# Order of issue in a fused attention, cond2 and ffn kernel: fixed delays replaced by a clock of estimates, with finer parts and layer norm by pairs

## Chip, cores and metric

The kernel runs on one core of one Trainium2 chip. The metric is the device time of one execution in microseconds (us). The engines are TensorE (PE; its weight loads are listed as PEld), VectorE (DVE), ScalarE (ACT), GpSimd (POOL) and SyncE (SP), which here only issues DMAs. [...]

## What is computed

The input `x` is [8, 512, 256] in float32: eight images of T = 512 tokens with C = 256 channels. Cut to what matters, the reference is:

```python
y  = x @ weight[itok].T + bias[itok]             # per image, one of 8 weight sets
q, k, v = silu(y @ Wq), silu(y @ Wk), y @ Wv     # 16 heads of 16
q, k = lrpe(q), lrpe(k)                          # [t*cos, t*sin], 32 per head
o  = (tril(q @ k.T) @ v) @ Wo                    # linear attention, causal, no softmax
x  = x + layernorm(o * sigmoid(y @ G1 @ G2)) * gamma + beta

ctx   = ema(x, tau_ctx)                          # cond2: running averages along T
gated = x * sigmoid([x, ctx] @ Wg.T + bg)
mod   = 0.5 + sigmoid(gelu(x @ Wn1.T + bn1) @ Wn2.T + bn2)
temporal = sum_d softmax(blend)_d * ema(gated * mod_d, tau_d)     # D = 8 traces
c  = layernorm((gelu(x @ Wsoma.T + bsoma) * sigmoid(temporal @ Wtemp.T + btemp)) @ Wout.T)
c  = c * gamma + beta

g, u = bitlinear(c, w_gate), bitlinear(c, w_up)  # ffn, INNER = 1024
x  = x + bitlinear(silu(g) * u, w_down)          # rows quantised to 8 bit, weights to -1, 0, 1
```

## The kernel before

One image is worked on by three Python generators, which issue instructions and yield between parts: `attention(b)` (L248), `cond2(b)` (L650) and `ffn(b)` (L845). Two more, `setup_cond2` (L512) and `setup_ffn` (L623), prepare constants and quantised weights at the start. A main loop (from L891) resumes one generator at a time; in the steady state the attention of image b, cond2 of image b−1 and the ffn of image b−2 are all running, so that their instructions are mixed on every engine.

The names that the profile shows:

- *attention*: `pxT` (x transposed), `py` (y), then for each of four tiles of 128 tokens `pkq` and `pv` (projections), `ktok` and `qtok` (the rotation, on POOL), `pkT`, `pqT` (transposed) and `pst` (chunk states, summed into `total` on DVE). For each pair of tiles there are two groups of `pe` (energies; DVE multiplies by the causal mask into `et`), `po` (output, copied to `aT`) and `pw` (times Wo). `pg` and `pgt` make the gate. Then the layer norm: `og`, `bn`, `mv` on DVE, `rstd` on POOL (L243, L244), L503 and `x` (L506) on DVE. POOL adds beta to x once, early (L444).
- *cond2*: `px2T`, the scan `cT` (L660), `ph`, `pso` (soma), `pm` (mod), `pwg` (gated), `pc`, `pr`, then `ptr`: two k parts for each of two groups of four traces, each in one four-bank tile of PSUM, summed into `tempT` by four DVE instructions. After it `ptg`, `pwo`, and on DVE the layer norm and quantisation of `c2` in two pairs of tiles: L808, L814, L819, L840, `c_inv`, `steps`, L827 and L830, which writes `cq`. SP transposes `cq` into `cqT` by DMA.
- *ffn*: for each of four tiles two groups of `pw_gateT` and `pw_upT` (L858), `sig` on ACT, `h` on DVE (L862), then `hmax` (L864), scales, L868 and `hq` (L870), a DMA transpose to `hqT`, `pd` (L885), `res` (L887) and the store.

PSUM holds four banks that all these tiles share in rotation (pool `ps`) and one four-bank tile (pool `ps_t`, tag `ptr`). The SBUF pools `p1` to `p6` have as many buffers per name as their number says.

What sets the order is a clock that counts PE's work by hand-written figures. Each generator yields the time at which its next part is ready, as a fixed delay after that:

```python
    def spent(work, then):
        now[0] += work
        return now[0] + then
    ...
        ripe = [r for r in running if running[r][0] <= now[0]]
        rank = min(ripe) if ripe else min(running, key=lambda r: running[r][0])
```

Among the ripe generators ffn goes first, then cond2, then attention. The attention of image b+1 starts once image b has issued its second `po` (`tail[b]`). The order in which the loop issues is, but for small moves by the framework below, the order on each engine.

Of the kernel before, what the change touches and what calls it, by code (L numbers as in the profile page):

```python
# [15 lines left out]
P = 128  # L16
# [14 lines left out]

@with_exitstack
def adaln_attn_ffn_kernel(ctx: ExitStack, tc: tile.TileContext, a: dict, out: bass.AP):
# [13 lines left out]
    cp = ctx.enter_context(tc.tile_pool(name="const", bufs=1))  # L47
    ps = ctx.enter_context(tc.tile_pool(name="ps", bufs=4, space=bass.MemoryType.PSUM))
    ps_t = ctx.enter_context(tc.tile_pool(name="ps_t", bufs=1, space=bass.MemoryType.PSUM))
    p1 = ctx.enter_context(tc.tile_pool(name="p1", bufs=1))  # L50
    p2 = ctx.enter_context(tc.tile_pool(name="p2", bufs=2))
    p3 = ctx.enter_context(tc.tile_pool(name="p3", bufs=3))
    p4 = ctx.enter_context(tc.tile_pool(name="p4", bufs=4))
    p6 = ctx.enter_context(tc.tile_pool(name="p6", bufs=6))
# [10 lines left out]
    now = [0.0]  # L65

    def spent(work, then):

        now[0] += work
        return now[0] + then  # L70
# [5 lines left out]
    nc.vector.tensor_copy(ident_bf, ident)  # L76
    ones = cp.tile([P, P], F32, name="ones")
    nc.vector.memset(ones, 1.0)
    minus_half = cp.tile([P, 1], F32, name="minus_half")
    nc.vector.memset(minus_half, -0.5)  # L80

    causal = cp.tile([P, 64], F32, name="causal")
    for r in range(2):
        nc.gpsimd.affine_select(
            out=causal[64 * r : 64 * (r + 1), :],
            in_=ones[64 * r : 64 * (r + 1), :64],
            pattern=[[1, 64]],
            compare_op=ALU.is_ge,
            fill=0.0,
            base=0,  # L90
            channel_multiplier=-1,
        )

    own = cp.tile([P, 2, 2, HD], F32, name="own")
    nc.vector.memset(own, 0.0)
    for j in range(4):
        nc.vector.memset(own[32 * j : 32 * (j + 1), j // 2, j % 2, :], 1.0)
# [3 lines left out]
    nc.sync.dma_start(sid_t, a["sid"].rearrange("(o n) -> o n", o=1))  # L101

    def load_input(b):
        xs = p4.tile([P, NT, C], F32, tag="x", name=f"x_{b}")
        nc.sync.dma_start(xs, x[b].rearrange("(t p) c -> p t c", p=P))
        sid = nc.sync.value_load(sid_t[0:1, b : b + 1], min_val=0, max_val=NS - 1)
        wt = p1.tile([P, KC, C], F32, tag="wt", name=f"wt_{b}")
        nc.sync.dma_start(
            wt,
            a["weightT"].rearrange("s (k p) o -> s p k o", p=P)[bass.ds(sid, 1)].rearrange("s p k o -> (s p) k o"),  # L110
        )
        bt = p2.tile([P, KC], F32, tag="bt", name=f"bt_{b}")
        nc.sync.dma_start(bt, a["biasT"][bass.ds(sid, 1)].rearrange("s p k -> (s p) k"))
        return xs, wt, bt
# [4 lines left out]
    def load_w(name, src, eng=nc.sync):  # L119
        rows, cols = src.shape  # L120
        t = cp.tile([P, rows // P, cols], F32, name=name)
        eng.dma_start(t, src.rearrange("(k p) n -> p k n", p=P))
        return t

    def load_row(name, src):
        t = cp.tile([P, src.shape[0]], F32, name=name)
        nc.sync.dma_start(t, src.partition_broadcast(P))
# [3 lines left out]
    nc.scalar.dma_start(theta_c, a["theta_c"])  # L131

    wkq = cp.tile([P, KC, 2, C], F32, name="wkq")
    for i, n in enumerate(("wk", "wq")):
        nc.scalar.dma_start(wkq[:, :, i, :], a[n].rearrange("(k p) n -> p k n", p=P))
    wv = load_w("wv", a["wv"], eng=nc.scalar)
# [3 lines left out]
    nc.vector.memset(g1, 0.0)  # L140
    nc.sync.dma_start(g1[:, :, :HD], a["g1"].rearrange("(k p) n -> p k n", p=P))
    g2 = cp.tile([64, C], F32, name="g2")
    nc.vector.memset(g2, 0.0)
    for u in range(2):
        nc.sync.dma_start(g2[32 * u : 32 * u + HD, :], a["g2"])
# [6 lines left out]
    nc.sync.dma_start(tau, a["taus"].partition_broadcast(P))  # L152
    blend = p1.tile([D, C], F32, tag="blend", name="blend")
    nc.sync.dma_start(blend, a["blend"])
    raws = {}

    def load_raw(n, *places):
# [3 lines left out]
            pool.tile([P, half * cols], F32, tag=tag, name=f"{n}_raw_{s}") for s, (pool, tag) in enumerate(places)  # L161
        ]
        for s, raw in enumerate(raws[n]):
            nc.sync.dma_start(
# [10 lines left out]
    for s in range(2):  # L175
        nc.sync.dma_start(w["wn2"][HN * s : HN * (s + 1), :], a["wn2T"])
        nc.sync.dma_start(w["bn1"][HN * s : HN * (s + 1), :], a["bn1"].rearrange("(p o) -> p o", o=1))
    w["bn2"] = load_row("bn2", a["bn2"])
    for n in ("bsoma", "btemp"):
        w[n] = cp.tile([P, KC], F32, name=n)  # L180
        nc.sync.dma_start(w[n], a[n])
# [13 lines left out]
    for g in range(NG):  # L195
        nc.vector.tensor_scalar(diag[:, g, :], ident, theta_c[:, g : g + 1], None, ALU.mult)
    theta = bank("theta")
    nc.tensor.matmul(theta, ones, diag.rearrange("p g n -> p (g n)"), start=True, stop=True)
    posn = p1.tile([P, NT], F32, tag="posn", name="posn")
    nc.gpsimd.iota(posn, pattern=[[P, NT]], base=0, channel_multiplier=1, allow_small_or_imprecise_dtypes=True)  # L200
    half_pi = cp.tile([P, 1], F32, name="half_pi")
    nc.vector.memset(half_pi, HALF_PI)
    ang = p1.tile([P, NT, H, HD], F32, tag="soma", name="ang")
    for t in range(NT):
        nc.vector.tensor_scalar(
# [8 lines left out]
    nc.vector.tensor_scalar(turns, ang, INV_TWO_PI, MAGIC, ALU.mult, ALU.add)  # L214
    nc.vector.tensor_scalar(turns, turns, -MAGIC, None, ALU.add)
    for part in (TWO_PI_1, TWO_PI_2, TWO_PI_3):
        nc.vector.scalar_tensor_tensor(ang, turns, -part, ang, ALU.mult, ALU.add)
    nc.vector.tensor_scalar(ang, ang, PI_BELOW, -PI_BELOW, ALU.min, ALU.max)
    nc.vector.scalar_tensor_tensor(turns, ang, -1.0, ang, ALU.mult, ALU.max)
    cs = cp.tile([P, NT, NG * P], F32, name="cs")  # L220
    cs_by_head = cs.rearrange("p t (h e d) -> p (t h) e d", e=2, d=HD)
    nc.scalar.activation(cs_by_head[:, :, 1, :], ang.rearrange("p t h d -> p (t h) d"), AF.Sin)
    nc.scalar.activation(
# [6 lines left out]
    for i in range(3):  # L230
        vz = cp.tile([P, 2, H // 2, 4, HD], F32, name=f"vz{i}")
        nc.gpsimd.memset(vz, 0.0)
        vz_bufs.append(vz)

    def layer_stats(src, mv_row):
        st = p3.tile([P, nc.vector.BN_STATS_DIM], F32, tag="bn", name="bn")
        nc.vector.bn_stats(st, src)
        nc.vector.bn_aggr(mv_row, st)

    def layer_rstd(mv, name):  # L240

        r = p2.tile([P, NT], F32, tag="rstd", name=name)
        nc.gpsimd.tensor_scalar(r, mv[:, :, 1], 4.0 * EPS, None, ALU.add)  # L243
        nc.gpsimd.tensor_tensor(r, r, minus_half.to_broadcast([P, NT]), ALU.pow)  # L244
# [3 lines left out]
    def attention(b, xs, wt, bt):  # L248

        xT = p1.tile([P, KC, T], F32, tag="xT", name=f"xT_{b}")  # L250
        for k in range(KC):
            pt = bank(f"pxT_{b}_{k}")
            for t in range(NT):
                nc.tensor.transpose(pt[:, chunk(t)], xs[:, t, chunk(k)], ident)
            nc.scalar.copy(xT[:, k, :], pt)
        yield spent(1.1, 1.4)
        yT = p1.tile([P, KC, T], F32, tag="yT", name=f"yT_{b}")
        for o in range(KC):
            py = bank(f"py_{b}_{o}")
            for k in range(KC):  # L260
                nc.tensor.matmul(py, wt[:, k, chunk(o)], xT[:, k, :], start=k == 0, stop=k == KC - 1)  # L261
            nc.scalar.activation(yT[:, o, :], py, AF.Identity, bias=bt[:, o : o + 1])  # L262
        wt_free[0] = b + 1
        yield spent(3.7, 1.0)

        kTs, qTs, vzs, sgs = {}, {}, {}, {}

        def project(t):
# [3 lines left out]
            for k in range(KC):  # L272
                nc.tensor.matmul(  # L273
# [3 lines left out]
            for k in range(KC):  # L277
                nc.tensor.matmul(pv, yT[:, k, chunk(t)], wv[:, k, :], start=k == 0, stop=k == KC - 1)  # L278
            sg = p2.tile([P, 2, H, HD], F32, tag="sg", name=f"sg_{b}_{t}")
            nc.scalar.activation(sg.rearrange("p e h d -> p (e h d)"), pkq, AF.Silu)  # L280
# [4 lines left out]
            nc.scalar.copy(vzs[tp][:, u, :, 0:4:3, :], pv.rearrange("p (a e d) -> p a e d", e=2, d=HD))  # L285
            sgs[t] = sg
# [4 lines left out]
        def rotate(t, i):  # L291
# [3 lines left out]
            tok = p3.tile([P, NG * P], F32, tag="tok", name=f"{n}tok_{b}_{t}")  # L295
            nc.gpsimd.tensor_mul(  # L296
                tok.rearrange("p (h e d) -> p h e d", e=2, d=HD),
                sgs[t][:, i].unsqueeze(2).to_broadcast([P, H, 2, HD]),
                cs[:, t, :].rearrange("p (h e d) -> p h e d", e=2, d=HD),
            )  # L300
            pt = bank(f"p{n}T_{b}_{t}")
            for g in range(NG):
                nc.tensor.transpose(pt[:, chunk(g)], tok[:, chunk(g)], ident)  # L303
            nc.scalar.copy(turned[:, :, chunk(u)], pt.rearrange("p (g n) -> p g n", n=P))  # L304
            return tok

        def states(t, tok):
# [4 lines left out]
            for g in range(NG):  # L312
                for r, hh in ((0, 0), (1, 1), (0, 1), (1, 0)):
                    rows = slice(64 * r, 64 * (r + 1))
                    cols = slice(P * g + 64 * hh, P * g + 64 * (hh + 1))
                    nc.tensor.matmul(  # L316
# [6 lines left out]
            for r in range(2):  # L323
                c = 2 * t + r
                if c:
                    sts[c] = p6.tile([P, NG, 2, 2 * HD], F32, tag="st", name=f"st_{b}_{c}")
                    nc.gpsimd.tensor_mul(  # L327
# [8 lines left out]
                if c:  # L336
                    nc.vector.tensor_add(new, src, total[0])  # L337
                else:
                    nc.vector.tensor_copy(new, src)
# [4 lines left out]
        def energies(tp, hh):  # L344
# [3 lines left out]
            for g in range(NG):  # L348
                for u in range(2):
                    for e, r in ((0, 0), (1, 1), (0, 1), (1, 0)):  # L350
                        rows = slice(32 * (2 * hh + e), 32 * (2 * hh + e + 1))
                        at = slice(P * u + 64 * r, P * u + 64 * (r + 1))
                        nc.tensor.matmul(  # L353
                            pes[e][64 * r : 64 * (r + 1), g, u, :], kT[rows, g, at], qT[rows, g, at], start=True, stop=True
                        )
            for e in range(2):
                et = p4.tile([P, NG, 2, 64], F32, tag="et", name=f"et_{b}_{tp}_{2 * hh + e}")
                nc.vector.tensor_mul(  # L358
# [6 lines left out]
        def output(tp):  # L365
# [7 lines left out]
            def out(half, pair, u, r, *factors, last):  # L373
                q = 32 * pair
                nc.tensor.matmul(po[r][q : q + 32, half, u, :], *factors, start=(r, q) not in begun, stop=last)  # L375
# [28 lines left out]
            for r in range(2):  # L404
                nc.scalar.copy(aTs[tp].rearrange("p h (u r n) -> p h u r n", u=2, r=2)[:, :, :, r, :], po[r])  # L405

        ready = {}

        def projected(t):
            project(t)  # L410
            ready[t] = spent(2.9, 1.6)

        def turned(t):
            tok = rotate(t, 0)
            states(t, tok)
            spent(1.3, 0)
            rotate(t, 1)
            ready[t] = spent(0.6, 1.2)

        projected(0)  # L420
        yield now[0]
        projected(1)
        yield ready[0]
        turned(0)
        yield now[0]
        projected(2)
        yield ready[1]
        turned(1)
        yield ready[1]
        energies(0, 0)  # L430
        at = spent(1.2, 0)
        yield at
        projected(3)
        yield max(at, ready[2])
        turned(2)
        energies(0, 1)
        at = spent(1.2, 2.0)
        yield max(at, ready[3])
        while b and not done[b - 1, "attention"]:
            yield now[0] + 1.0  # L440
        output(0)
        turned(3)

        nc.gpsimd.tensor_add(xs, xs, beta_a.unsqueeze(1).to_broadcast([P, NT, C]))  # L444
        spent(2.0, 0)
        yield now[0]

        pg = bank(f"pg_{b}")[:64, : T // 2]
        for tp in range(NT // 2):
            for k in range(KC):  # L450
                for u in range(2):
                    nc.tensor.matmul(
# [7 lines left out]
        nc.scalar.copy(g1T, pg)  # L460
        at = spent(1.1, 0.8)
# [538 lines left out]
```

## Time and profile before

| what | value |
|---|---|
| median of the runs | 779.91 us |
| lowest, highest of 3 | 776.56, 782.77 us |
| the profiled execution | 779.86 us |
| its span, first to last instruction | 778.2 us |
| mean granted clock of TensorE | 0.930 |
| busy: PE, DVE, ACT, POOL | 665.8, 505.7, 260.5, 196.7 us |
| DMA | 28.64 MB, mean 37 GB/s |

The span is what the views divide; 1.66 us of the execution lie around it. The line PEclk cuts the span in 40 slices of 19.5 us and gives the granted clock in tenths (9 is 90% or more). A row of a waits view names the waiting engine with its tile and line, what it waited for, and then the total in us, the number of times and the longest. A row of the timeline gives the start, the duration, the instruction and, in brackets, how long its engine had been idle before it and what ended that.

### The profile page before, as it was taken

The numbers are of one execution on the slowest core, as the hardware profiler recorded it, in microseconds if no ns is written. First come the engines' busy times: TensorE is split into PE (matmuls) and PEld (weight loads), VectorE is DVE, ScalarE is ACT, GpSimd is POOL, SyncE is SP. The second block draws the span as 40 slices with busy tenths as digits, with TensorE's granted clock in tenths as the row PEclk, the third lists the DMA queues.
The fourth block names the chain that finished last, engine by engine and source line by source line (L and its number), as shares of the span: only waits on it lengthen the run. The fifth ranks groups of instructions, "written<-read, shape, count | busy, mean of one in ns | idle before, by whom it ended". The sixth has DMA issues, their size and how long they took to land.

```text
span 778.2 us, 21224 instructions
## 1 busy us (share of the span) xinstructions
PE 665.8 (86%) x9330; PEld 445.2 (57%) x9330; DVE 505.7 (65%) x1047; ACT 260.5 (33%) x480; POOL 196.7 (25%) x223
## 2 busy tenths in 40 slices
PE   2988999799888999799888999799988999795644
PEld 1566666566664666566664666466764667454312
DVE  3896355785567665775658753776658755785565
ACT  2822343243224333253234332253234333240111
POOL 3542252114301251023311152113411252110000
PEclk7969999999999999899999999999999999898756
DMA  6700000021001210022001210021000200021011
GB/s 229 231 3 3 14 2 4 15 67 56 4 16 32 56 37 3 15 63 60 4 15 21 69 35 4 16 49 48 3 16 6 69 9 3 16 55 28 1 41 54
DMA packets 61198, 28.64 MB, mean 37 GB/s; under 512 B 46346, under 2 KB 60594, under 8 KB 61106
## 3 DMA queue, kind: packets, MB, share of 16 engines
q1 hardware_dynamic: 60146, 26.50, 12.8%
q8 instruction: 73, 1.20, 0.6%
q10 hardware_dynamic: 960, 0.79, 0.3%
q14 instruction: 19, 0.16, 0.1%
HBM read 12.60 MB, written 4.19 MB: 22 GB/s over the span
## 4 chain that ended last, share of the span: by engine, by line
PE 67%; DVE 18%; issue 5%; ACT 4%; DMA 3%; POOL 3%; ACTq 0%; POOLq 0%; DVEq 0%; SPq 0%
PE pkq L273 7%; PE pwg L710 7%; PE ptr L760 5%; PE po L375 5%; PE ptg L778 4%; PE pso L682 4%; PE pv L278 3%; PE pd L885 3%; PE pe L353 3%; PE pwo L803 3%; PE pst L316 3%; PE py L261 3%; PE pw L491 2%; PE pqT L303 2%; PE pkT L303 2%
## 5 line engine op out<-in xcount | busy, mean ns | idle before, releaser
L765 DVE SCALAR_TENSOR_TENSOR tempT<-ptr,bw_c,tempT 128x512 f32<-128x512 f32 x128 | 95.8, 748 | 41.8 <-PE ptr L760 39.1
L861 ACT ACTIVATE sig<-pw_gateT,steps 128x512 f32<-128x512 f32 x64 | 43.2, 687 | 80.5 <-PE pw_gateT L858 45.9
L296 POOL TENSOR_TENSOR ktok<-sg,cs 128x512 f32<-128x512 f32 x32 | 41.2, 1286 | 108.2 <-ACT sg L280 94.9
L858 PE MATMUL pw_gateT<-w_gateT,cqT 128*128 128x512 bf16 x128 | 40.3, 398 | 31.4 <-DVE h L862 24.7
L273 PE MATMUL pkq<-wkq,yT 128*128 128x512 f32 x128 | 64.2, 622 | 0.3 <-ACT yT L262 0.3
L858 PEld LDWEIGHTS <-cqT 128*128 128x128 bf16 x256 | 25.9, 101 | 64.6 <-issue 35.9
L862 DVE SCALAR_TENSOR_TENSOR h<-pw_upT,steps,sig 128x512 f32<-128x512 f32 x64 | 45.9, 744 | 15.2 <-ACT sig L861 8.8
L375 PE MATMUL po<-et,vz 64*32 64x64 f32 x2048 | 32.0, 246 | 25.0 <-DVE et L358 15.7
L327 POOL TENSOR_TENSOR st<-total,own 128x256 f32<-128x256 f32 x56 | 41.2, 752 | 48.1 <-DVE total L337 48.1
L760 PE MATMUL ptr<-dm,gated 32*128 32x128 f32 x1024 | 40.6, 293 | 10.7 <-DVE tempT L765 10.7
L358 DVE TENSOR_TENSOR et<-pe,causal 128x512 f32<-128x512 f32 x64 | 41.8, 685 | 12.2 <-PE pe L353 12.2
L296 POOL TENSOR_TENSOR qtok<-sg,cs 128x512 f32<-128x512 f32 x32 | 40.8, 1277 | 32.7 <-PE pst L316 32.5
L885 PE MATMUL pd<-w_downT,hqT 128*128 128x256 bf16 x256 | 35.9, 288 | 14.5 <-DMA hqT<-hq 14.5
L760 PEld LDWEIGHTS ptr<-dm,gated 32*128 32x128 f32 x1024 | 33.9, 194 | 21.5 <-issue 19.5
L375 PEld LDWEIGHTS po<-et,vz 64*32 64x32 f32 x2048 | 25.0, 114 | 32.4 <-DVE et L358 19.0
L353 PE MATMUL pe<-qT,kT 32*64 32x64 f32 x2048 | 41.6, 223 | 1.3 <-ACT qT L304 0.9
L858 PE MATMUL pw_upT<-w_upT,cqT 128*128 128x512 bf16 x128 | 41.5, 408 | 1.3 <-ACT sig L861 1.3
L353 PEld LDWEIGHTS pe<-qT,kT 32*64 32x64 f32 x2048 | 35.7, 135 | 10.9 <-issue 4.1
L887 DVE SCALAR_TENSOR_TENSOR res<-pd,hstep,x 128x256 f32<-128x256 f32 x32 | 15.4, 482 | 40.7 <-PE pd L885 40.7
L885 PEld LDWEIGHTS <-hqT 128*128 128x128 bf16 x256 | 25.8, 103 | 27.5 <-DMA hqT<-hq 19.4
L405 ACT COPY aT<-po 128x256 f32<-128x256 f32 x32 | 10.5, 375 | 91.6 <-PE po L375 91.6
L864 DVE TENSOR_REDUCE hmax<-h 128x1 f32<-128x1024 f32 x32 | 38.9, 1216 | 0.3
(201 smaller groups left out, 1338.6 us busy)
## 6 DMA issues: line engine op xcount, KB each, us to landing
x<-in_x_dram SPq DMA_DIRECT2D x8, 512.0 KB, 4.3
out_dram<-res SPq DMA_DIRECT2D x32, 128.0 KB, 1.7
wt<-in_weightT_dram SPq DMA_DIRECT2D x8, 256.0 KB, 2.8
w_gateT_raw<-in_w_gateT_dram SPq DMA_DIRECT2D x2, 512.0 KB, 6.7
w_upT_raw<-in_w_upT_dram SPq DMA_DIRECT2D x2, 512.0 KB, 7.9
w_downT_raw<-in_w_downT_dram SPq DMA_DIRECT2D x2, 512.0 KB, 7.5
wgT<-in_wgT_dram SPq DMA_DIRECT2D x1, 512.0 KB, 8.7
hqT<-hq SPq DMA_TRANSPOSE x32, 2.7
```

The source lines that it names most:

```text
L273: nc.tensor.matmul(pkq, yT[:, k, chunk(t)], wkq[:, k].rearrange("p e c -> p (e c)"), start=k == 0, stop=k == KC - 1)
L296: nc.gpsimd.tensor_mul(tok.rearrange("p (h e d) -> p h e d", e=2, d=HD), sgs[t][:, i].unsqueeze(2).to_broadcast([P, H, 2, HD]), cs[:, t, : ...
L353: nc.tensor.matmul(pes[e][64 * r : 64 * (r + 1), g, u, :], kT[rows, g, at], qT[rows, g, at], start=True, stop=True)
L358: nc.vector.tensor_mul(et.rearrange("p g u n -> p (g u) n"), pes[e].rearrange("p g u n -> p (g u) n"), causal.unsqueeze(1).to_broadcast([P ...
L375: nc.tensor.matmul(po[r][q : q + 32, half, u, :], *factors, start=(r, q) not in begun, stop=last)
L710: nc.tensor.matmul(pwg[:, u, :], src[:, k % KC, chunk(t + u)], w["wgT"][:, k, :], start=k == 0, stop=k == 2 * KC - 1,)
L760: nc.tensor.matmul(ptr[:, r, :, t, :], gated[rows, t, chunk(k)], dm[rows, t], start=True, stop=True)
L765: nc.vector.scalar_tensor_tensor(acc, ptr[:, :, e].rearrange("p r t n -> p r (t n)"), w["bw_c"][:, k, d + e : d + e + 1], acc, ALU.mult, A ...
L858: nc.tensor.matmul(pm, cqT[:, t, k, :], w[n][:, k, cols], start=k == 0, stop=k == KC - 1)
L861: nc.scalar.activation(sig, pgu[0], AF.Silu, scale=steps[:, 0, t : t + 1])
L862: nc.vector.scalar_tensor_tensor(h[:, cols], pgu[1], steps[:, 1, t : t + 1], sig, ALU.mult, ALU.mult)
L885: nc.tensor.matmul(pd, hqT[:, k, :], w["w_downT"][:, k, :], start=k == 0, stop=k == KI - 1)
```

## The change

The computation stays as it is. `spent` and the fixed delays go. A class `Clock` estimates, for every instruction as it is issued, when it will start and end: it keeps a time for each engine (with the gaps left in it), for each area of each tile (last write and last use), for each buffer that a new tile takes over, for the DMA queue, for ACT's function tables[...]. `Engine` and `Pool` wrap the engines and the pools so that each call is accounted. A generator now yields a function that the main loop asks anew each time:

```diff
-    now = [0.0]
-    def spent(work, then):
-        now[0] += work
-        return now[0] + then
+    def needs(*aps, banks=(ps, "ps"), when=lambda: True):
+        def ready():
+            return max([clock.when(v) for v in aps] + [banks[0].free(banks[1])]) if when() else None
+        return ready
...
+        now = clock.at["tensor"]
+        ready = {r: v for r, v in ((r, running[r][0]()) for r in running) if v is not None}
+        ripe = [r for r in ready if ready[r] <= now]
+        rank = min(ripe) if ripe else min(ready, key=ready.get)
```

The ranks stay. The parts get finer: the turning of a tile in a k and a q part, `ptr` one k at a time, `ptg` and `pso` one output half at a time, `pwo` one pair of tiles at a time, `inner` (it was `hidden`) one group of gate and up at a time. In attention, the rotations follow at once on the projection (pool `p3` becomes `p4`), the layer norm is done by pairs of token tiles, and the first pair's `pw` stands ahead of the second `po`:

```diff
+            for i, n in enumerate("kq"):
+                toks[t, i] = tok = p4.tile([P, NG * P], F32, tag="tok", name=f"{n}tok_{b}_{t}")
+                gp.tensor_mul(
...
-        energies(1, 1)
-        yield spent(1.2, 2.0)
-        output(1)
-        at = spent(2.0, 0.9)
-        tail[b] = True
+        yield needs(kTs[1], qTs[1])
+        energies(1, 1)
         og = p1.tile([P, NT, C], F32, tag="og", name=f"og_{b}")
-        mv = p2.tile([P, NT, 2], F32, tag="mv", name=f"mv_{b}")
         for tp in range(NT // 2):
             t = 2 * tp
             if tp == 1:
-                yield at
+                yield needs(ets[1, 1, 1], sts[7])
+                output(1)
+                tail[b] = True
+            yield needs(aTs[tp])
...
+            mv = p2.tile([P, 2, 2], F32, tag="mv", name=f"mv_{b}_{t}")
...
-        rstd = layer_rstd(mv, f"rstd_a{b}")
-        for t in range(NT):
+            rstd = layer_rstd(mv, f"rstd_a{b}_{t}")
+            for u in range(2):
```

The next attention starts from the gate (`head[b]`, set once `pg` is copied) and waits for the tail only before it turns its second tile:

```diff
+        ac.copy(g1T, pg)
+        head[b] = True
...
-        if b < B and b in loaded and tail[b - 1]:
+        if b < B and b in loaded and head[b - 1]:
...
+        yield needs(toks[1, 0], when=lambda: tail[b - 1])
+        yield from turned(1)
```

In cond2 the products `dm` (L749) are issued next to `modt`, ahead of `gated`. In ffn the transpose to `hqT` follows directly on `hq`:

```diff
-            hqs[t] = hq, hstep, spent(2.1, 6.0)
...
-            hq, hstep, at = hqs.pop(t)
-            yield at
-            hqT = p2.tile([P, KI, P], BF, tag="hqT", name=f"hqT_{b}_{t}")
-            nc.sync.dma_start(hqT, hq, transpose=True)
-            yield spent(0.0, 4.0)
+            hqT = p2.tile([P, KI, P], BF, tag="hqT", name=f"hqT_{b}_{t}")
+            sy.dma_start(hqT, hq, transpose=True)
+            hqs[t] = hqT, hstep
...
+            hqT, hstep = hqs.pop(t)
+            yield needs(hqT)
```

Loops that polled for another generator (`while not ...: yield now[0] + 1.0`) become the `when` of such a function. In the two setups `paced` functions, which wait for DVE's estimate to come near, take the place of the fixed delays, and `blend` shares a buffer with `square`.

## The prediction

> **What bounds the kernel now.** I read section 1 of the page, then the windows for the three stages, then PE's waits, then the timeline of one turn of the steady stage.
>
> ```profile
> PE 665.8 (86%) x9330; PEld 445.2 (57%) x9330; DVE 505.7 (65%) x1047; ACT 260.5 (33%) x480; POOL 196.7 (25%) x223
> PEclk7969999999999999899999999999999999898756
> ...
> PE 67%; DVE 18%; issue 5%; ACT 4%; DMA 3%; POOL 3%; ACTq 0%; POOLq 0%; DVEq 0%; SPq 0%
> ```
>
> TensorE (PE) is busy 86% of the span, and the chain that ended last runs 67% on it; VectorE (DVE) comes next with 65% and 18%. The stages differ, which the windows show (PE, PEld, DVE, ACT, POOL busy, then clock, DMA share, GB/s):
>
> ```profile
> 0.00:144.00 144.00, 119.80 (x1990) 82.19 (x1991) 89.42 (x198) 53.33 (x100) 49.76 (x64) 0.92 0.22 68
> 144.00:672.00 528.00, 481.36 (x6986) 327.19 (x6985) 348.09 (x717) 184.74 (x342) 140.80 (x150) 0.96 0.12 29
> 672.00:778.00 106.00, 64.60 (x357) 35.87 (x355) 68.14 (x136) 22.41 (x38) 6.09 (x9) 0.78 0.13 33
> ```
>
> From the first gate matmul of image 0 (144) to that of image 6 (672) there are six turns of 88.0 us, in each of which one image's attention, another's cond2 and a third's ffn are mixed. PE idles 528.0 − 481.4 = 46.6 us there, 7.8 per turn. Eleven windows of 3.41 us at half clock cost at most 18.6 us of work, 3.1 per turn. So a turn holds 88.0 − 7.8 − 3.1 = 77.1 us of PE work at full clock: an order of issue has 10.9 us per turn to win, and any amount to lose. What PE waits for:
>
> ```profile
> PE pw_gateT L858 <- DVE h L862: 24.7, 7, 3.5
> PE po L375 <- DVE et L358: 15.7, 9, 1.9
> PE pd L885 <- DMA hqT<-hq: 14.5, 3, 6.7
> PE ptr L760 <- DVE tempT L765: 10.7, 5, 3.4
> PE po L375 <- issue: 9.5, 9, 2.3
> ```
>
> The first is one stall per turn, and the timeline shows its place:
>
> ```profile
> 588.94 0.37 POOL L243 TENSOR_SCALAR rstd_a<-mv 128x4 f32<-128x4 f32 x1 [12.40 <-DVE mv L238]
> 589.39 1.04 POOL L244 TENSOR_TENSOR rstd_a<-rstd_a,minus_half 128x4 f32<-128x4 f32 x1
> 590.46 1.28 DVE L506 SCALAR_TENSOR_TENSOR x<-og,rstd_a,x 128x256 f32<-128x256 f32 x3 [1.24 <-POOL rstd_a L244]
> ...
> 592.05 0.75 DVE L862 SCALAR_TENSOR_TENSOR h<-pw_upT,steps,sig 128x512 f32<-128x512 f32 x1
> ...
> 592.85 0.59 PE L858 MATMUL pw_gateT<-w_gateT,cqT 128*128 128x512 bf16 x2 [3.53 <-DVE h L862]
> ```
>
> DVE takes its instructions in order. The first h stands behind the whole layer norm of four token tiles, and PE has no bank until h is done: 3.53 us. The hqT and tempT waits belong to head and tail; per turn the rest is 1.93 for the second po (behind et) and some 2.3 in small pieces.
>
> [...] windows of 3.41 us at 0.5, after stalls of 1.7 to 3.5 us. [...] the scan L660 takes 1.20 to 1.22 us alone and 2.39 beside POOL's add of beta to x, which takes 2.36:
>
> ```profile
> L444 POOL TENSOR_TENSOR x<-x,beta_a x8: 2337/2360/2369, 13.1 to 595.4; 128x1024 f32<-128x1024 f32 x8
> ...
> L660 DVE TENSOR_TENSOR_SCAN cT<-alpha,x2T x16: 1200/1218/2390, 80.8 to 685.6; 128x512 f32<-128x512 f32 x16
> ```
>
> **The change part by part.** The computation stays; only orders change. I read them, instruction by instruction and per engine, from the built programs. A turn's end of cond2 and start of ffn after the change is followed here from the last ptr group (t = 0, times in us).
>
> 1. *PE up to ffn.* New order: pqT 1.1, pg to 1.7, pe to 2.7, pgt to 3.8; ptg needs tempT and DVE's four adds (4 × 0.78 = 3.1), 4.83 to 8.36; pe to 9.4; pw of the first pair (1.65) to 11.1; twelve pwo (2.8) to 13.9; 22 of po, four pwo, the rest of po to 18.0; the next image's pxT (0.97) to 19.0; pw of the second pair to 20.65. Two stalls of before are gone: po finds et done at 11.1 (saves 1.93), and h no longer stands behind four tiles (saves 3.53 and some clock).
>
> 2. *DVE, which decides the rest.* Before, the quantisation of c2 ran ahead of the whole layer norm: the first cq transpose was out at 579.12, the last landed by 583.7, and the gate matmul came at 586.49 after PE's own work, so the DMA was hidden by nearly 3 us. Now the first layer-norm pair stands ahead of c2. et ends at 11.1; the pair runs 11 to 14.6 (og 0.34, bn 0.33 and mv 0.11 each twice, POOL's rstd 1.0, L503 and L506 0.4 each twice); then L808 for the first pair, L814 twice, L819, L808 again at 17.2 and two L814 before the chain L840, c_inv, steps, L827 twice, L830: the first cq ends at 20.5. The transpose takes 2.42 to land: 22.95. PE has been done since 20.65: a new stall of 2.3.
>
> 3. *Ffn's start.* Gate at 22.95; sig; first h 24.4 to 25.05. In DVE's queue h_0 stands before the second mv, so mv, rstd and x of the second pair follow at 25.15 to 27.15; second h 27.85, hmax (1.13) 29.6, two h of the second tile to 30.2, then the cT scan, L868, the other hmax and hq, 34.15. The hqT transpose lands after 2.73: 36.9. Between gate and pd, PE now has four gate/up groups (3.5), px2T (1.0) and py (3.5): 8 us of work in 14. Idle 6.1. Before, pd came at 604.28, 17.8 us after the gate, with ph (1.1) and pso (3.7) as further cover; these two now stand behind pd.
>
> 4. *Smaller stalls.* The first ptr of the second half waits for tempT with two totals between on DVE: +0.83. "Issue" gaps and the rest keep about 1.3. Sum of idle 2.3 + 6.1 + 0.83 + 1.3 = 10.5 instead of 7.8. Half clock: stalls are fewer but the 6 us one is long; I take 2.3 (bounds 1 and 3.4) instead of 3.1. A turn: 77.1 + 10.5 + 2.3 = 89.9, +1.9.
>
> 5. [...] Attention of the next image starts from the gate on, so its pxT comes at 18 to 19 and POOL's 2.36 us add of beta to x starts there. Before, it started at 595.4 and hit the scan. Now it falls on L827 and L830 of c2, on the path to cqT. [...] L503 took 1.87 instead of 0.47 where this add met it in the head. I take 2.1: +4.0 per turn.
>
> 6. *What I cost at nothing.* Rotations on POOL right after projection, and dm moved ahead of gated: POOL is 25% busy and the waiters come later; they would cost if a rotation waited for sg behind something, at most the 1.28 of one. ACT gets four table loads per turn instead of two; [...] the trace shows 1.28; ACT is 33% busy, so 2.56 is hidden, and if not it adds up to 2.6. The rstd in pairs costs POOL two small extra instructions (under 1 us), inside step 2. Issuing hqT directly after hq moves no transfer past another: SP's order in the steady stage stays. The one added condition (the second tile's turning waits for the tail of the attention before) holds only the next attention back; it orders issue and puts no wait in an engine's queue.
>
> 7. *Head (0 to 144).* The setup of the ffn weights is spread by DVE's estimate and no longer stands before the first et: I count −4 of PE's 24 idle us there; [...] Net −2 (±4).
>
> 8. *Tail (672 on).* ptr of image 7 ends 37.0 after the gate of image 6 before and, by the steps above, 41.5 after: +4.5 (±3). What follows is one image alone, in the order it had.
>
> Sum: −2 + five turns at 4.0 + one at 1.9 (no image is left to add beta to) + 4.5 = +24.4. Against the profiled execution's own 779.86 (span 778.2, 1.66 around it) that is 804. The median of the runs is 779.91, so nothing is to be shifted.
>
> **The rivals.**
> *It wins (other side).* The stalls of before are gone and nothing comes in their place: h and et save 5.5 idle and about 1 of clock per turn, if cq is early enough. Point from which it decides: cqT lands before the second pw ends (20.65), and hqT before py is through. For it: 3.5 and 1.9 us are real and sit on PE. Against: my DVE sum makes cq 2.3 late. All of it over six turns, 39, with the head's 4 would give 737; I take half, since something else is always late next: 779.9 − 21.5 = 758.
> [...] DVE's c2 operations slip past the add, or meet it elsewhere: turns of +1.9, 11.4 + 4.5 − 4 = +12, 792. For it: a shift of 2 us suffices. Against: both start from the same pw_2 neighbourhood every turn.
> *The bubbles only move.* Finer parts let PE find work in most of the 6 us and stalls come to before's 7.8: 780. For it: the order's finer grain; against: the order is fixed and named in step 3.
>
> **How the numbers follow.** Main case 0.45 (804, own range 796 to 815); [...] bubbles move 0.16 (772 to 786); it wins 0.16 (750 to 772). The range leaves out the upper tail and part of the winning case: 768 to 815. About 1% (7.8 us) is what a measurement of this kernel tells from no change. Faster by more: 0.16; within: 0.16; slower: 0.68 [...].
>
> **What would show each step right or wrong.** In the profile after: PE's wait of po for et and of the gate for h gone (step 1); a wait of the gate for DMA cqT of about 2 to 4 each turn (2, 5); a wait of pd_0 for DMA hqT of 4 or more each turn (3); a DVE L827 or L830 of 2 us beside the x add (5); turns of 92 between gate matmuls of neighbouring images. Wrong if cqT is no waiter on the list, or if turns are under 88.

## The result and the profile after

The changed kernel takes 828.57 us (median of 4, 825.88 to 828.73) beside 780.46 for the kernel before in the same runs: a ratio of 1.0597, 95% interval 1.056 to 1.0634. It is 6% slower; the forecast was 3%, and the time lies outside its range. The profiled execution took 825.88 us with a span of 824.2, which is 46.0 more than before.

Every call goes through the recording helper, so all lines of the changed kernel are L167, and rows are told apart by their tiles. The head of the page, with section 4:

```profile
PE 672.1 (82%) x9315; PEld 438.3 (53%) x9330; DVE 528.7 (64%) x1047; ACT 273.1 (33%) x492; POOL 209.6 (25%) x239
PEclk9979899989999999899998999999997999979767
...
PE 43%; DVE 22%; issue 7%; DMA 5%; ACT 2%; POOL 1%; another core or an unknown queue 1%; POOLq 0%; DVEq 0%; ACTq 0%; SPq 0%
```

PE's busy time grew by only 6 us, but its share of the chain that ended last fell from 67% to 43%. PE now waits inside the loop. Its waits:

```profile
PE pd L167 <- DMA hqT<-hq: 47.9, 10, 7.5
PE pw_gateT L167 <- DMA cqT<-cq: 35.6, 8, 7.0
PE ptr L167 <- DVE tempT L167: 13.4, 10, 3.4
...
PE px2T L167 <- DVE x L167: 4.5, 2, 3.4
```

Before, the gate matmul waited 24.7 us for h and po 15.7 for et. Of these two, 0.6 us for h is left; hqT and cqT stand in their place with 47.9 + 35.6 = 83.5, against 14.5 + 6.6 = 21.1 before, where the row for cqT was

```profile
PE pw_gateT L858 <- DMA cqT<-cq: 6.6, 1, 6.6
```

The stages, cut at the first gate matmul of images 0, 6 and 7, add up to the whole:

| stage | before | after | difference | forecast |
|---|---|---|---|---|
| head, to the gate of image 0 | 144.1 | 156.1 | +11.9 | −2 |
| six turns, to the gate of image 6 | 527.9 | 553.1 | +25.2 | +21.9 |
| to the gate of image 7 | 71.8 | 80.3 | +8.6 | |
| the rest | 34.4 | 34.7 | +0.3 | together +4.5 |

One turn in the timeline, from the layer norm's first pair to the first pd:

```profile
515.99 0.88 DVE L167 SCALAR_TENSOR_TENSOR x<-og,rstd_a,x 128x256 f32<-128x256 f32 x2 [0.60 <-POOL rstd_a L167]
...
516.79 0.68 DVE L167 TENSOR_TENSOR c<-pwo,gamma_c 128x512 f32<-128x512 f32 x1
...
520.81 2.71 DVE L167 TENSOR_SCALAR c<-c,c_inv 128x256 f32<-128x256 f32 x2
520.81 2.55 POOL L167 TENSOR_TENSOR x<-x,beta_a 128x1024 f32<-128x1024 f32 x1 [1.40 <-PE pxT L167]
...
524.47 2.89 SPq L167 DMA_TRANSPOSE cqT<-cq  x2
...
526.95 0.39 PE L167 MATMUL pw_gateT<-w_gateT,cqT 128*128 128x512 bf16 x1 [4.49 <-DMA cqT<-cq]
...
538.29 4.00 SPq L167 DMA_TRANSPOSE hqT<-hq  x2
...
541.10 1.19 PE L167 MATMUL pd<-w_downT,hqT 128*128 128x256 bf16 x6 [4.11 <-DMA hqT<-hq]
```

c2 starts only after the pair's x. Its scaling (L827 before) takes 2.71 us for two instructions, about as long as POOL's add of beta beside it (2.55); cq is out late, and the gate waits 4.49. Then pd waits 4.11; the ph and pso that stood ahead of it before, as cover, now stand behind it.

### The profile page after: what moved, and what is told of

It is laid out like the page before. It is cut to its first block, busy times and chain, and to the rows that moved or that the text cites. A ratio compares the mean times of both kernels' runs of the same rounds, so it can differ in the third digit from the quotient of the medians.

```text
span 824.2 us, 21253 instructions
## 1 busy us (share of the span) xinstructions
PE 672.1 (82%) x9315; PEld 438.3 (53%) x9330; DVE 528.7 (64%) x1047; ACT 273.1 (33%) x492; POOL 209.6 (25%) x239
## 4 chain that ended last, share of the span: by engine, by line
PE 43%; DVE 22%; issue 7%; DMA 5%; ACT 2%; POOL 1%; another core or an unknown queue 1%; POOLq 0%; DVEq 0%; ACTq 0%; SPq 0%
PE pwg L167 6%; DVE tempT L167 4%; PE pkq L167 4%; PE ptr L167 4%; DVE hmax L167 4%; DVE h L167 3%; DVE c L167 3%; DMA hqT<-hq 3%; PE ptg L167 3%; PE pd L167 3%; PE pw_upT L167 3%; PE pw_gateT L167 3%; DMA cqT<-cq 2%; PE po L167 2%; PE pv L167 2%
## 5 line engine op out<-in xcount | busy, mean ns | idle before, releaser
L167 DVE SCALAR_TENSOR_TENSOR tempT<-ptr,bw_c,tempT 128x512 f32<-128x512 f32 x128 | 95.9, 750 | 47.9 <-PE ptr L167 44.3
L167 POOL TENSOR_TENSOR ktok<-sg,cs 128x512 f32<-128x512 f32 x32 | 41.0, 1281 | 215.4 <-ACT sg L167 201.7
L167 ACT ACTIVATE sig<-pw_gateT,steps 128x512 f32<-128x512 f32 x64 | 43.3, 686 | 125.4 <-PE pw_gateT L167 71.7
L167 PE MATMUL pd<-w_downT,hqT 128*128 128x256 bf16 x256 | 40.5, 312 | 47.9 <-DMA hqT<-hq 47.9
L167 PE MATMUL pw_gateT<-w_gateT,cqT 128*128 128x512 bf16 x114 | 47.2, 495 | 36.2 <-DMA cqT<-cq 35.6
L167 PEld LDWEIGHTS <-cqT 128*128 128x128 bf16 x256 | 30.2, 121 | 80.6 <-DMA cqT<-cq 38.4
L167 PE MATMUL pkq<-wkq,yT 128*128 128x512 f32 x128 | 67.6, 642 | 5.4 <-DVE res L167 4.4
L167 DVE SCALAR_TENSOR_TENSOR h<-pw_upT,steps,sig 128x512 f32<-128x512 f32 x64 | 46.6, 746 | 36.1 <-PE pw_upT L167 21.9
L167 POOL TENSOR_TENSOR st<-total,own 128x256 f32<-128x256 f32 x56 | 43.5, 790 | 100.3 <-DVE total L167 99.4
L167 PEld LDWEIGHTS <-hqT 128*128 128x128 bf16 x256 | 27.1, 109 | 69.2 <-DMA hqT<-hq 55.8
L167 PE MATMUL ptr<-dm,gated 32*128 32x128 f32 x1024 | 42.7, 300 | 14.6 <-DVE tempT L167 13.4
L167 ACT ACT_TABLE_LOAD x36 | 46.2, 1283 | 17.8 <-PE pkq L167 12.7
L167 PE MATMUL pw_upT<-w_upT,cqT 128*128 128x512 bf16 x127 | 49.3, 478 | 1.4 <-issue 0.7
L167 DVE TENSOR_TENSOR gated<-pwg,bg 128x512 f32<-128x512 f32 x16 | 11.1, 691 | 59.4 <-PE pwg L167 59.4
L167 PEld LDWEIGHTS ptr<-dm,gated 32*128 32x128 f32 x1024 | 35.3, 199 | 25.8 <-issue 20.4
L167 PEld LDWEIGHTS pe<-qT,kT 32*64 32x64 f32 x2048 | 36.5, 135 | 17.1 <-issue 11.2
L167 DVE TENSOR_TENSOR et<-pe,causal 128x512 f32<-128x512 f32 x64 | 40.9, 680 | 6.3 <-PE pe L167 6.3
L167 POOL TENSOR_TENSOR qtok<-sg,cs 128x512 f32<-128x512 f32 x32 | 44.4, 1387 | 0.0
L167 PE MATMUL pe<-qT,kT 32*64 32x64 f32 x2048 | 42.3, 224 | 0.1
L167 POOL TENSOR_SCALAR rstd_a<-mv 128x2 f32<-128x2 f32 x16 | 6.0, 374 | 141.3 <-DVE mv L167 141.3
L167 DVE TENSOR_REDUCE hmax<-h 128x1 f32<-128x1024 f32 x32 | 38.8, 1214 | 0.4
L167 PE MATMUL pwo<-woutT,soma 128*128 128x256 f32 x128 | 31.7, 388 | 4.8 <-ACT square L167 3.7
```

Of the source, the lines that this page charges most:

```text
L167: made = issue(*args, **kw)
```

## The experiments

In all but e1 and e6 the loop takes the parts from a list instead of choosing by the clock. Without an edit that list is the changed kernel's own order. Ratios are to the kernel before, run beside it; the changed kernel's is 1.0597. In the lists of parts, `in` is one group of gate and up, a number names the tile or the first tile of the pair (`po_1` is the second po), `n.` is the attention of the next image, and `|` only divides the list.

**e1_no_beta: the scaling of c2 without POOL's add of beta.**

```diff
-        gp.tensor_add(xs, xs, beta_a.unsqueeze(1).to_broadcast([P, NT, C]))
+        clock.account("gpsimd", "tensor_add", (xs, xs, beta_a.unsqueeze(1).to_broadcast([P, NT, C])), {})
```

> The changed kernel without POOL's add of beta to x (beta is left out of the result); the planner's clock still counts it, so the order on every engine is the same. [...] the pair of L827-type scalings that takes 2.7 us beside the add falls to 0.6, cq is out 2.1 earlier, the gate's wait for cqT falls from 4.5 to about 2.4, each turn from 92.2 to about 90.1, and in the head px2T and cqT come 2 to 4 earlier: 828.6 to about 812. Rival (the add is harmless, cqT is late because of the first layer-norm pair alone): the wait stays at 4 or more and the time within 3 us of 828.

815.87 us, ratio 1.0396 (1.0345 to 1.0447). The scaling and the gate in its timeline:

```profile
514.42 0.61 DVE L167 TENSOR_SCALAR c<-c,c_inv 128x256 f32<-128x256 f32 x2
...
518.46 0.60 PE L167 MATMUL pw_gateT<-w_gateT,cqT 128*128 128x512 bf16 x2 [2.44 <-DMA cqT<-cq]
```

The pair takes 0.61 instead of 2.71, and the wait falls by 2.05, from 4.49 to 2.44, near the forecast's 2.1 for the add and 2.3 without it. The changed kernel itself has the same case once, at the gate of image 6, where no later image is left to add beta to:

```profile
709.20 0.39 PE L167 MATMUL pw_gateT<-w_gateT,cqT 128*128 128x512 bf16 x1 [2.46 <-DMA cqT<-cq]
```

A turn gains less than the wait does. The median is 12.7 us lower, of 16 expected (15.7 by the ratios), but between the profiled executions (825.88 and 818.63 us) the six turns fall only from 553.1 to 550.3 us, 0.5 a turn instead of 2.1. Part of the gain comes back at once, since px2T now waits up to 1.5 for h in each turn (6.7 us instead of 2.1), and PE's busy time in these turns is 2.3 us longer. The head gains 3.9.

**e2_ln_after_c2: the first pair behind c2.** In turn b, by the names of parts:

```diff
- ... pgt ptg ptg pe  pw_0 pwo pwo | po_1 pxT pw_2 | in in in in px2T ...
+ ... pgt ptg ptg pe       pwo pwo | po_1 pxT pw_0 pw_2 | in in in in px2T ...
```

> The changed kernel with the second po ahead of the first pair's pw, so that on DVE the quantisation of c2 stands ahead of both layer-norm pairs; the order of parts is otherwise written down as the changed kernel has it. Theory of the sum (the first pair is 2.3 of the 4.5 us[...]): the wait for cqT falls to 0 to 2 per turn, but the whole layer norm is then ahead of h again and px2T, and costs 2 to 4 per turn in waits for h or x: turn 90 to 92, total 815 to 829. Rival (putting the pair ahead of c2 is the main loss): turns fall by 4.5 to under 88, total about 800.

831.40 us, ratio 1.0615 (1.0563 to 1.0666): no better than the change. PE's waits:

```profile
PE pd L167 <- DMA hqT<-hq: 46.6, 10, 7.6
PE pw_gateT L167 <- DMA cqT<-cq: 17.1, 7, 6.6
...
PE px2T L167 <- DVE h L167: 10.9, 7, 1.6
...
PE pw_gateT L167 <- DVE h L167: 5.0, 7, 0.8
PE pw_upT L167 <- DVE og L167: 4.4, 6, 1.7
```

The time lies just above the theory's range, and its rival is refuted. The wait for cqT falls by 18.5 us, and waits for h and og behind the layer norm take its place: in the six turns PE idles 71.5 us, as in the changed kernel (71.4). Which of the two stands first in DVE's queue decides the name of the wait, and hardly its length.

**e3_fill_hqT: ph and half of pso ahead of the first pd.**

```diff
- in in in in px2T py pd_0 in in ph pso pd_1 ...
+ in in in in px2T py ph pso pd_0 in in pd_1 ...
```

> The changed kernel with one edit of the written order: ph and the first half of pso are issued ahead of the first pd. Theory (the wait for hqT is a hole that has lost its cover): ph 1.0 and half of pso 1.9 take 2.9 of the 4.1 us wait away in each of six turns, turn 92.2 to about 89.3, total about 811. Rival (the wait is made by DVE and only moves on to the next wait): turn still above 91.5, total 824 to 829.

825.54 us, ratio 1.0534 (1.0473 to 1.0595), too near the change to be told from it; the second theory was right. The three pd of one turn that follow each other:

```profile
449.67 1.05 PE L167 MATMUL pd<-w_downT,hqT 128*128 128x256 bf16 x8 [1.14 <-DMA hqT<-hq]
452.47 1.05 PE L167 MATMUL pd<-w_downT,hqT 128*128 128x256 bf16 x8
462.44 0.72 PE L167 MATMUL pd<-w_downT,hqT 128*128 128x256 bf16 x5 [2.90 <-DMA hqT<-hq]
```

The first pd's wait shrinks from 4.1 to 1.1, but the work moved ahead of it is missing ahead of the third, which waits 2.9. Over the kernel PE waits 49.2 us for hqT, against 47.9. In the six turns PE idles 65.6 us instead of 71.4, but is busy 4.3 us longer, so little of that reaches the time. Cover that is taken from the same stretch mostly moves the wait.

**e5_head_setup: the setup of w_down earlier.** Parts of `setup_ffn` are "q":

```diff
- ... pe pw_0 pxT po_1 q py q pw_2 pkq pkq q px2T ...
+ ... q q q pe pw_0 pxT po_1 py pw_2 pkq pkq px2T ...
```

> The changed kernel with only the head changed: the last three parts of the ffn weights' setup (w_down) are issued ahead of the first image's last energies instead of after its second po. Theory (the head lost 12 us, 3 to 6 of them because the w_down instructions stand ahead of the first layer norm on DVE): px2T of image 0 starts 3 to 6 us earlier and the whole is 822 to 826. Rival [...]: under 1.5 us, 827 to 829.

825.78 us, ratio 1.0533 (1.0472 to 1.0593). By the whole it can't be told from the change; by the stage it can. In the changed kernel's head DVE waited for PE's sum of w_down and then did its six instructions ahead of the first og:

```profile
72.20 0.16 DVE L167 TENSOR_SCALAR wstep<-pwsum 128x1 f32<-128x1 f32 x1 [6.46 <-PE pwsum L167]
...
76.52 0.75 DVE L167 SCALAR_TENSOR_TENSOR og<-gate,pw 128x256 f32<-128x256 f32 x2
```

With the edit PE's wait for x falls from 4.5 to 0.5, and the gate of image 0 comes at 151.2 instead of 156.1, as the first theory had it; the rival held x to be late through POOL's rotations beside it alone. Of these 4.9 us the profiled execution loses 3.5 again in its six turns, whose order is unchanged.

**e6_before_ln_pairs: the kernel before, with the layer norm by pairs alone.**

```diff
-        mv = p2.tile([P, NT, 2], F32, tag="mv", name=f"mv_{b}")
...
+            mv = p2.tile([P, 2, 2], F32, tag="mv", name=f"mv_{b}_{t}")
...
-        rstd = layer_rstd(mv, f"rstd_a{b}")
-        for t in range(NT):
+            rstd = layer_rstd(mv, f"rstd_a{b}_{t}")
+            for u in range(2):
```

> The kernel before with one part of the change alone: the layer norm of attention by pairs of token tiles (mv and rstd per pair); fixed delays, parts and order of PE stay. The first h then stands ahead of the second pair's L503 and x on DVE. Theory (the 3.5 us wait of the gate for h is DVE's order alone): the wait falls to under 2 us per turn, 10 to 14 us in all: about 768. Rival (DVE is behind by the same amount of work, and the wait only changes its name, px2T waiting for x): within 4 us of 780.

783.61 us, ratio 1.0046 (1.0009 to 1.0084): no gain, as the second theory had it.

```profile
PE pxT L254 <- DVE h L862: 9.8, 6, 1.6
...
PE pw_gateT L858 <- DVE h L862: 5.5, 7, 0.8
```

The wait of the gate for h falls from 24.7 to 5.5 us, and pxT waits 9.8 for h. PE's idle time per turn falls only from 7.8 to 7.3 us on average, and the time doesn't follow.

**e7_tail_order: the turn of image 6.**

```diff
- in in in in px2T ph pso pd_0 in in pd_1 in in pso pd_2 pm pwg pd_3 pwg pc ...
+ in in in in px2T ph pso pso pm pd_0 in in pwg pd_1 pwg pc in in pr ptr pd_2 pd_3 ...
```

> The changed kernel with only the turn of image 6 reordered: soma, mod and gated of image 7 are issued between the ffn parts of image 6 ahead of its pd, as cover, instead of after them. Theory (the tail's 9 us are the wait for hqT of image 6, 9.2 instead of 1.1, which the finer parts put ahead of cond2's work): the wait falls under 3 us and the last two stages take 5 to 9 us less: 820 to 824. Rival (the tail is bound by the chain over tempT and by half clock): under 2 us, 827 to 829.

813.95 us, ratio 1.0382 (1.0309 to 1.0456): 14.6 us less than the changed kernel, more than either theory had. PE's waits from the gate of image 6 to that of image 7, first of the changed kernel, then of this one:

```profile
PE ptr L167 <- DVE tempT L167: 10.1, 3, 3.4
PE pw_gateT L167 <- DMA cqT<-cq: 9.5, 2, 7.0
PE pd L167 <- DMA hqT<-hq: 9.2, 2, 5.1
```

```profile
PE pw_gateT L167 <- DMA cqT<-cq: 9.5, 2, 7.0
PE ptr L167 <- DVE tempT L167: 6.7, 2, 3.4
PE pd L167 <- DMA hqT<-hq: 4.4, 2, 2.7
```

This stage falls from 80.3 to 68.5 us, below the 71.8 of before. The wait for hqT stays at 4.4, where the first theory had under 3. More is won elsewhere: cond2 of image 7, whose chain over ptr ends the program, no longer stands behind ffn parts that wait, and those parts fill one of the three waits for tempT.

**e8_dve_cover: an order for DVE's queue.** The parts are those of the changed kernel, but for the second po, which stands ahead of both pw, and the next attention may start at any time. The head and the turn of image 6 are ordered anew too. A turn:

```diff
+ in in in in px2T ph pso pso pkT pqT pd_0 in in pd_1 in in pm pwg pwg pd_2 pd_3
+ pc pkq_2 pr ptr pkT pqT pe ptr pkq_3 ptr pkT pqT pe ptr n.pxT po_0 pkT pqT ptg ptg pg pe pwo pwo
+ pgt pe n.py po_1 pw_0 pw_2 n.pkq_0 n.pkq_1
```

> The finer parts of the changed kernel in a written order made for DVE's queue: c2 is quantised ahead of the layer norm, and PE's work that needs nothing from DVE (py and the first two projections of the next attention, soma, the first turning) is spent where DVE runs behind, between the second pw and the gate matmuls and between those and pd; pxT, and with it POOL's add of beta, comes earlier, beside ptr. Theory (the loss of the change is where the parts stand in DVE's queue and what PE has left as cover, not the finer parts or the early attention): the waits of the gate and of pd fall under 2 us per turn each, turn 79 to 83, total 730 to 755. Rival (DVE is the bound of a turn, or the finer parts cost by themselves): turn 86 or more, total 775 or more.

767.37 us, ratio 0.9807 (0.9742 to 0.9872): 1.9% under the kernel before, with an interval below 1, though by less than expected. In the turns cqT delays PE no longer, et in one of six, hqT by 1.6 at most, but the third gate/up group waits for h:

```profile
PE pd L167 <- DMA hqT<-hq: 24.5, 10, 6.8
PE pw_upT L167 <- DVE h L167: 16.4, 6, 2.8
...
PE pw_gateT L167 <- DMA cqT<-cq: 7.0, 1, 7.0
```

Of the rows shown, only 3.4 of hqT's 24.5 and nothing of cqT's lie in the turns. Five turns are 83 to 88 us, between the two theories; the sixth, which has no next attention to begin, is 76.4. All six take 508.1 us instead of the changed kernel's 553.1, the head 148.9 instead of 156.1. So the finer parts and the early start of the next attention do not by themselves make the loss; the order in which they were put does, of which e2 shows that the place of the second po is not the cause alone. No run corrected the estimates of the clock, so why it chose its order stays open.

**e9_more_cover and e10_rotations_away.** e9 moves more cover to where e8 still waits, and takes the image-6 turn of e7; e10 then moves py and two projections of the next attention ahead of the second po:

```diff
- in in in in px2T ph pso pso pkT pqT pd_0 ...               (e8)
+ in in pkT pqT in in px2T ph pso pso pkq_2 pd_0 ...         (e9)
...
- ... pwo pwo n.py po_1 pw_0 pw_2 n.pkq_0 n.pkq_1            (e9)
+ ... pwo pwo n.py n.pkq_0 n.pkq_1 po_1 pw_0 pw_2 n.pkT n.pqT  (e10)
```

> The written order of the run before (e8) with more cover: the first turning stands between the second and third gate/up group, where PE waited 2.7 us for h, the third projection ahead of the first pd, the turning of the second tile ahead of pr, both last energies ahead of pwo; and the turn of image 6 as in e7. Theory (a turn is bound by PE's 77 us of work plus what DVE leaves uncovered): the 2.7 us wait falls under 1, the last two stages are 5 us shorter, total 745 to 760. Rival (DVE's queue sets when h and hq come, so cover only moves the wait to pd or ptr): turns stay at 85, only the tail gains, 760 to 766.

756.00 us, ratio 0.9651 (0.9617 to 0.9686). The time lies in the range of the first theory, but not for its reasons. As the second had it, the 2.7 us wait for h stayed, under another name (pst, 16.2 us in all), and five turns are 83.4 to 86.8 us; and the last two stages, which both theories had shorter, take 106.4 us as in e8 (106.5). What was won, 8.7 us, lies in the six turns. The timeline shows why the wait stayed:

```profile
576.25 1.27 POOL L167 TENSOR_TENSOR ktok<-sg,cs 128x512 f32<-128x512 f32 x1
576.32 2.90 DVE L167 SCALAR_TENSOR_TENSOR x<-og,rstd_a,x 128x256 f32<-128x256 f32 x2 [0.90 <-POOL rstd_a L167]
577.48 1.45 POOL L167 TENSOR_TENSOR qtok<-sg,cs 128x512 f32<-128x512 f32 x1
```

Two x take 2.90 us, instead of 0.88 in the turn of the changed kernel shown above, beside the rotations of the projections that were meant as cover.

> The order of e9 with py and the next attention's first two projections ahead of the second po instead of behind pw, so that their four rotations on POOL run beside the quantisation of c2 and not beside the layer norm, where pairs of L503 and x took 1.9 and 2.9 us instead of 0.86 and 0.88; the first turning follows pw. Theory [...]: the wait falls under 1 and a turn by 2 or more, total 740 to 750. Rival ([...] h waits for the layer norm all the same): 753 or more.

751.18 us, ratio 0.9603 (0.9565 to 0.9641), the best of all, 4% under the kernel before, and just above the theory's range. The head of its page and two of its waits:

```profile
PE 652.0 (87%) x9330; PEld 430.8 (58%) x9330; DVE 532.0 (71%) x1047; ACT 257.1 (34%) x478; POOL 205.5 (27%) x239
PEclk7999999999999999999999999999999999998757
...
PE ptr L167 <- DVE tempT L167: 11.0, 11, 3.4
...
PE ph L167 <- DVE h L167: 5.0, 6, 0.8
```

The wait for h is 0.8 a turn. Five turns are 81.5 to 84.1 us, on average 82.8 after 85.0 in e9, and the sixth is 72.4. All six take 486.5 us, against 527.9 in the kernel before; the head, with more of the next attention in it, gives 13.3 us of that back (157.5 instead of 144.1). The rotations now run beside the scaling of c2 and the `steps` ahead of it, and these take longer there (two scalings 2.79 us instead of 0.61 in e1, `steps` 1.24 instead of 0.14 in the changed kernel's turn):

```profile
478.47 1.24 DVE L167 TENSOR_TENSOR steps<-amax,wstep 128x4 f32<-128x4 f32 x1
479.63 2.79 DVE L167 TENSOR_SCALAR c<-c,c_inv 128x256 f32<-128x256 f32 x2
479.65 1.28 POOL L167 TENSOR_TENSOR qtok<-sg,cs 128x512 f32<-128x512 f32 x1
481.00 1.27 POOL L167 TENSOR_TENSOR ktok<-sg,cs 128x512 f32<-128x512 f32 x1
```

There the second po, both pw and a turning (some 9 us) still stand ahead of the gate, so that costs PE nothing in five of the six turns.

## Why the prediction was right in kind and wrong in size

*Step 1, right.* The waits of po for et are gone, and that of the gate for h but for 0.6 us in the last image. In the kernel before, the turn's first h had its `sig` at 587.82 and started at 592.05, behind the x in DVE's queue.

*Steps 2 and 5, right as to the wait, shown by e1.* Forecast 2.3 for the pair and 2.1, an estimate, for POOL's add beside the scaling, 4.4 together; measured 4.5 in most turns, of which 2.05 goes with the add. That all of the 2.1 reaches the length of a turn is not shown.

*Step 3, right in place, too large.* Forecast 6.1 a turn for pd and px2T. Measured in the six turns are 24.5 us for pd, 4.1 in each, and 2.1 for px2T in two of them, 4.4 a turn together. That this was lost cover alone is refuted by e3: the wait moves with the cover.

*Step 4, too small, and part of the sum is luck.* For the six turns:

```profile
156.00:709.00 553.00, 481.70 (x6964) 314.86 (x6976) 366.66 (x714) 196.37 (x352) 148.48 (x161) 0.95 0.11 28
```

PE idles 553.0 − 481.7 = 71.3 us (71.4 when cut exactly at the gates). Without cqT (23.9), pd and px2T (26.6) and tempT (2.2, 0.4 a turn instead of 0.83), 18.6 us are left for "issue" gaps and small pieces, 3.1 a turn where 1.3 was taken; pkq, which waits 0.7 a turn for `res`, is one that the prediction does not name. So what steps 3 and 4 took too high for hqT, px2T and tempT, 12.8 us, and too low for the rest, 10.8, nearly cancel: that the idle time comes near its forecast (six times 10.5 and five times 2.1, 73.5) is luck. For the half clock 2.3 a turn was taken, as an estimate, and so was the 1 us a turn that the winning case adds for it. PE's busy time, 80.3 a turn, is 3.2 above the estimate of 77.1, so the term was 0.9 a turn too small, if that estimate holds; the windows at half clock amount to 50.8 us, at most 50.8 / 2 / 6 = 4.2 a turn. The windows of 3.41 us that the prediction saw after stalls of 1.7 to 3.5 us are in the trace, but the length of a stall does not tell whether one follows: in the kernel before, a wait of 1.68 us at 474.0 was followed by one, and the 3.53 at 592.85 was not. With all this the six turns gave +25.2 for +21.9.

*Step 6, right in the turns, wrong in the head.* ACT has 36 table loads of 1.28 us instead of 24, as counted, and no wait of PE for ACT in the turns is longer than 0.7 us. Not counted was that DVE's instructions take longer beside the rotations too. In the turns it is hq of the fourth tile (1.65 us at 555.87, instead of 0.68 for the first tile), for which no pd waits; in the head it is x (1.90 us for two at 79.78 and 2.90 at 84.70, instead of 0.88), for which px2T does.

*Step 7, the one that failed most: head −2, measured +11.9.* The −2 was 4 won at the setup and 2 lost to POOL's add of beta, both estimates. Of the 21.6 us between the forecast of +24.4 and the measured +46.0, 13.9 lie here, 4.3 in step 8 and 3.3 in the turns. The 4.1 of po for et did go, as credited. Not seen were the wait for cqT, which the head ends with like every turn (4.7; only the 2 for the add were counted), the third `total` behind the quantisation of w_gate (+3.5), px2T behind that of w_down and behind the x that run beside rotations (4.5 instead of 1.6; e5 takes 4.0 of it away), more "issue" gaps of po (+1.3), and pxT of image 2, which is now in the head (+1.0). These are 13.4 on the losing side and 4.1 on the other, 9.3 in all. The 2.6 that stay unassigned are no wait: PE is busy 123.8 us in the head instead of 119.9, of which the pxT explains 1.0. I took the setup for work that had merely moved out of et's way, and did not ask what it stands in front of now.

*Step 8, the term of the tail: +4.5, measured +8.8.* In the turn of image 6 hqT costs 9.2 instead of 1.1: the 4.1 of the first pd, which step 3 has, and 5.1 of a later one, which no step names; e7 shows that the order of the parts in this one turn is the whole of it and more.

*The rivals.* The second rival (792, given 0.23) did not come, since the add met the scaling, which took 2.71 us; the bubbles didn't merely move within a change of the order, they grew; the winning side failed at the point named, since cqT lands after the second pw. Forecast and rivals shared one gap: none had the head on the losing side.

## What to carry to other kernels

When a scheduler's order changes, follow each engine's queue through the first and the last turn too: the stages that run once cost 20.7 of the 46 us here. A wait that DVE's queue made was not removed by reordering the same instructions around it (e2, e3, e6). It went when PE got work from outside that stretch (e8 to e10); these three changed the order of DVE's queue and the head as well, so the share of the cover alone is not separated. And whatever the cover triggers elsewhere, here rotations on POOL beside which two x took 2.90 us instead of 0.88, counts as part of its price.

## What the runs showed of the hardware

Instructions of DVE took longer beside some of POOL's, and not beside the add of beta alone. Beside that add the scaling of c took 2.71 us for two instructions, instead of 0.61 without it (e1). Beside rotations two x took 2.90 us instead of 0.88 (e9, and the changed kernel's turn), and even `steps`, with at most four elements per partition, took 1.24 instead of 0.14 (e10, and the changed kernel's turn). In each of these cases DVE was done when POOL's instructions beside it were, or up to 0.3 us later. Not every instruction took longer: in the kernel before, two bn took 0.74 us beside the add that starts at 73.19, as they do alone (0.75), and the L503 that follows took 1.87 instead of 0.45. What decides between these cases is not shown.

The windows at half clock, worked out from mean clock and span, fell from about 124 us in the changed kernel (0.925 over 824.2 us) to about 66 in e10 (0.956 over 748.4). PE's busy time fell with them, from 672 to 652 us for the same matmuls: 20 of the 75.8 us between the two spans.
